# Adding products of zeros to TensorE's message sums in 47 steps of a graph network kernel

## The chip, the core and the metric

The kernel runs on one core of one Trainium2 chip. The metric is the device time of one execution in microseconds (us). The core has five engines with queues of their own: TensorE (PE in the profile, with its weight loads as PEld), VectorE (DVE), ScalarE (ACT), GpSimd (POOL) and SyncE (SP). Engines wait for each other by semaphores.

## What is computed

The reference is one message passing block (PaiNN) on a graph of 1250 nodes with 512 features and 40000 edges, sorted by destination, then a residual addition and a layer norm:

```python
x_j = x[src]
v_j, s_j = x_j[:, :384].reshape(E, 128, 3), x_j[:, 384:]
s_j = silu(s_j @ W1 + b1) @ W3 + b3
edge_basis = rbf * cutoff @ W2 + b2
split = s_j * edge_basis
s1, s2, s3 = split[:, :128], split[:, 128:256], split[:, 256:]
v_msg = v_j * s1[:, :, None] + s3[:, :, None] * edge_attr1[:, None, :]
x = x + segment_sum(concat([v_msg, s2]), dst)
...
x = x + segment_sum(msg, dst)
return layernorm(x_in + x)
```

The first sum runs over messages of edges. For the second one, each node's message is made once per node, and the sum over edges is a product with a matrix of link counts, which the kernel gathers on the way.

## The kernel before

A table of 640 numbers per node is made first and kept in DRAM. Then the function `windowed` goes over the edges in batches of up to 4 x 128, some 80 steps of one batch each; four batches make a group, and a group's sums cover a window of 128 rows of destinations. For a batch, GpSimd gathers 128 rows four times (L782), three steps ahead. A step does the following.

- `messages(t)` on DVE: the one-hot matrix `hot` (L877) from `eb`, then the products of gathered rows and edge factors (L949, and L952 as the last reader of `eb`), with `spread` (L891) between them, then `pair` (L968).
- `add_messages(t - 1)` on TensorE: for each of the four tiles j a product of `hot` and the messages into rows 32j to 32j + 31 of the PSUM bank `agg` (L984), then twelve smaller products with `spread` (L990). In the changed kernel these are L987 and L998.
- `count_links(t - 1)` on TensorE: four f16 products of `one` and `pair` (L1013), 160 columns each, into the bank `adj`. The accumulator carried between groups comes in by L1005.
- `edge_factors(t + 1)` on TensorE: the edge factors of the next batch into `eb` (L938, four f32 products of 388 columns, eight records in the trace). There is one bank set `eb`, so this waits until DVE has read the last one.
- `gather(t + 3)`, the gathers for three steps on, whose first waits for `eb`.

Between these, tables (`first`, `early`, `late`, `dve`, `mid`, `amid`), filled by `at(when, step, rank, fn)`, put the work on finished groups and nodes: copying sums (`close_group`), joining two groups (`sum_block`, L1080), the node update (`times_u`, L1148, whose result ScalarE copies as `vu`; `times_uv`, L1159; `over_parts`, L1175), the basis transposes (L855) and the second sum (`begun`, L1388). Each engine works through its own list in the order in which the code issues it. The work repeats every eight steps, two groups being one block of nodes. Steps count from 0; the first starts some 30 us into the span.

The code around the change, in `add_messages`:

```python
for j in js:
    nc.tensor.matmul(
        agg[j * WIN : (j + 1) * WIN, :], hots[t][:, j, :],
        msg[:, j, :width], start=(i == 0), stop=False, skip_group_check=True,
    )
for c in range(3):
    for j in js:
        nc.tensor.matmul(
```

`sh.number` is an f16 tile of 128x256 that holds 0 to 255 in each row; `WIN` is 32 and `P` is 128.

Of the kernel before, what the change touches and what calls it, by code (L numbers as in the profile page):

```python
# [12 lines left out]
F16 = mybir.dt.float16  # L13
# [8 lines left out]
P = 128  # L22
# [18 lines left out]
WIN = SHARE + 2 * MARGIN  # L41
# [9 lines left out]
GROUP = 4  # L51
LEAD = 3
LAG = 2


def by_component(ap):
# [8 lines left out]
def gnn_resnorm(  # L65
# [31 lines left out]
    nc = tc.nc  # L97
# [8 lines left out]
    sh = Shared()  # L106
# [6 lines left out]
    const = ctx.enter_context(tc.tile_pool(name="const", bufs=1))  # L113
# [147 lines left out]
    for k in range(2):  # L261
# [4 lines left out]
        sh.number, pattern=[[1, 2 * P]], base=0, channel_multiplier=0,  # L266
        allow_small_or_imprecise_dtypes=True,
    )
    sh.basis = const.tile([P, TPC * CPG, FEAT], F32, name="basis")
    nc.gpsimd.memset(sh.basis[:, :, N_RBF:], 0.0)  # L270
    nc.gpsimd.memset(sh.basis[:, :, N_RBF], 1.0)
# [360 lines left out]
def windowed(tc, sh):  # L632
# [13 lines left out]
    nc = tc.nc  # L646
# [24 lines left out]
    def tiles(g, i):  # L671
        return [j for j in range(CPG) if lanes(g, i, j)]
# [14 lines left out]
    def last_tile(g, j):  # L687
        return max(i for i in range(TPC) if lanes(g, i, j))
# [7 lines left out]
    with tc.tile_pool(  # L696
        name="msg", bufs=4
    ) as pool, tc.manual_schedule(), ExitStack() as banks:

        number = sh.number  # L700
# [277 lines left out]
        def add_messages(t):  # L978
            g, i = batches[t]
            if i == 0:  # L980
                aggs[g] = ps_sum.tile([P, width], F32, name="agg")
            agg, msg, js = aggs[g], msgs.pop(t), tiles(g, i)
            for j in js:
                nc.tensor.matmul(  # L984
                    agg[j * WIN : (j + 1) * WIN, :], hots[t][:, j, :],
                    msg[:, j, :width], start=(i == 0), stop=False, skip_group_check=True,
                )  # L987
            for c in range(3):
                for j in js:
                    nc.tensor.matmul(  # L990
                        agg[j * WIN : (j + 1) * WIN, c * C : (c + 1) * C],
                        spread[t][:, j, c, :], msg[:, j, width:],
                        start=False, stop=(i == last_tile(g, j) and c == 2),
                        skip_group_check=True,
                    )
# [752 lines left out]
        for t in range(max(*first, *early, *late, *dve, *mid) + 1):  # L1748
            if t < NT:
                messages(t)  # L1750
            if t == NT - 4:
                assert all(len(tiles(*batches[u])) == CPG // 2 for u in range(NT - 3, NT))
                made_in[NT - 3], made_in[NT - 2] = new_banks("halves", [CPG // 2] * 2)
                made_in[NT - 1] = made_in[NT - 3]
            if t == NT - 1:
                out_banks.update(zip(in_factors, new_banks("out", [1] * CPG), strict=True))
            run(first, t)
            if 1 <= t <= NT:
                add_messages(t - 1)
                if t not in behind:  # L1760
                    count_links(t - 1)
            run(early, t)
            if t + 1 < NT - 2:
                made = edge_factors(t + 1)
            if t + 1 in (NT - 3, NT - 2):
                edge_factors(t + 2)
            if t + ahead < NT:
                gather(t + ahead, made if t + ahead < NT - 2 else None)
            if t in behind:
                count_links(t - 1)  # L1770
            run(mid, t)
            run(late, t)
            run(dve, t)
# [38 lines left out]
def _general(ctx, tc, sh):  # L1812
# [170 lines left out]
    def edge_sums(table, sums, begin, finish, add, pool, ps_agg):  # L1983
# [13 lines left out]

        for step in range(NT + LAG):
            t = step
            if t < NT:  # L2000
# [9 lines left out]
                nc.vector.tensor_scalar(hots[t], lane, slots[:, t, 4:5], None, op0=ALU.is_equal)  # L2010
            t = step - LAG
            if t >= 0:
# [134 lines left out]
```

## Time and profile before

| what | value |
|---|---|
| median of 3 runs | 572.19 us (569.93 to 572.43) |
| the profiled execution | 573.55 us |
| its span, first to last instruction | 571.7 us |
| mean granted TensorE clock in it | 0.881 of 2.4 GHz |
| PE busy | 456.2 us (80%), 4260 matmuls |
| DVE, ACT, POOL busy | 424.5 us, 380.3 us, 336.2 us |
| moved by DMA | 123.29 MB, mean 216 GB/s |

The span is what the trace covers; the execution's time has a little more around it. A busy share is an average over the whole span. In a timeline row the number after the start is the time from the start of the first merged instruction to the end of the last, "xN" counts the merged instructions, and the bracket gives the engine's idle time before the first one and what ended it. "issue" means that the profile shows nothing that ended it. The granted clock is what the throttle allowed TensorE, as a share of full speed.

### The profile page before, as it was taken

What the parts mean: (1) busy time and instruction counts of PE and PEld (TensorE: products, weight loads), DVE (VectorE), ACT (ScalarE), POOL (GpSimd) and SP (SyncE); (2) the same over time, 40 slices, a digit from 0 to 9 for tenths busy, and PEclk for the clock granted to TensorE, in tenths of its full rate; (3) what the DMA queues carried; (4) which work ended last, traced back from release to release, by engine and by line L of the source; (5) the groups of instructions that cost most, each with busy time, mean ns of one, the idle gap of its engine ahead of it and who ended that gap; (6) DMA issues with size and microseconds to landing.
All of it is one profiled execution on the core that took longest, in us unless ns stands there. A gap on an engine that the chain in (4) does not pass through costs nothing.

```text
span 571.7 us, 11259 instructions
## 1 busy us (share of the span) xinstructions
PE 456.2 (80%) x4260; PEld 256.5 (45%) x4260; DVE 424.5 (74%) x672; ACT 380.3 (67%) x976; POOL 336.2 (59%) x363
## 2 busy tenths in 40 slices
PE   9556787887878798687888788798879697899993
PEld 6322343453444354344534444454445364455672
DVE  6785877767876777687777877777767867797775
ACT  4675467485767657577856767695749566787664
POOL 8375656656655665666566665656555655664530
PEclk9757787878979887988889898999879998989998
DMA  8896777777777677777677778777766776877414
GB/s 267 288 284 180 214 229 217 218 217 228 212 234 200 222 211 200 239 216 210 204 243 213 236 223 235 203 229 239 234 196 201 214 206 204 253 214 230 178 37 148
DMA packets 37840, 123.29 MB, mean 216 GB/s; under 512 B 7141, under 2 KB 9815, under 8 KB 37779
## 3 DMA queue, kind: packets, MB, share of 16 engines
q0 software_dynamic: 25568, 104.34, 61.3%
q1 hardware_dynamic: 11010, 17.51, 9.5%
q8 instruction: 35, 0.57, 0.4%
q10 hardware_dynamic: 1200, 0.66, 0.4%
q14 instruction: 27, 0.21, 0.1%
HBM read 112.97 MB, written 9.51 MB: 214 GB/s over the span
## 4 chain that ended last, share of the span: by engine, by line
PE 70%; ACT 10%; DVE 9%; issue 9%; DVEq 0%; another core or an unknown queue 0%; ACTq 0%
PE eb L938 14%; PE agg L984 13%; PE agg L990 8%; PE adj L1013 5%; PE begun L1388 4%; ACT one L913 3%; PE work L1080 3%; PE work L855 3%; PE work L1175 2%; DVE more L952 2%; PE work L1159 2%; DVE nodes L952 2%; ACT one L903 2%; PE work L1224 1%; DVE more L949 1%
## 5 line engine op out<-in xcount | busy, mean ns | idle before, releaser
L782 POOL DMA_INDIRECT more<-table,src_i x189 | 184.7, 977 | 118.6 <-issue 42.7
L782 POOL DMA_INDIRECT nodes<-table,src_i x124 | 120.9, 975 | 79.6 <-issue 28.7
L913 ACT ACTIVATE one<-one,weight,src_f 128x128 f16<-128x128 f16 x313 | 128.5, 482 | 0.2
L938 PE MATMUL eb<-w_sb,basis_t 25*128 25x388 f32 x614 | 80.6, 584 | 58.7 <-issue 43.7
L903 ACT ACTIVATE one<-number,low 128x128 f16<-128x128 f16 x313 | 99.8, 392 | 16.6 <-PE adj L1013 10.0
L877 DVE TENSOR_TENSOR hot<-lane,eb 128x128 f32<-128x128 f32 (+1 forms) x78 | 22.1, 284 | 101.5 <-PE eb L938 61.5
L952 DVE TENSOR_TENSOR more<-more,eb 128x1536 f32<-128x1536 f32 (+2 forms) x48 | 81.8, 1705 | 0.0
L984 PE MATMUL agg<-more,hot 128*32 128x512 f32 x378 | 65.2, 704 | 2.6 <-issue 1.9
L938 PEld LDWEIGHTS eb<-w_sb,basis_t 25*128 25x128 f32 x614 | 27.0, 195 | 81.0 <-issue 59.8
L949 DVE TENSOR_TENSOR more<-more,eb 128x1024 f32<-128x1024 f32 (+2 forms) x48 | 56.9, 1186 | 2.5 <-issue 2.5
L990 PEld LDWEIGHTS agg<-more,spread 128*32 128x32 f32 x1134 | 41.9, 122 | 34.1 <-issue 32.9
L952 DVE TENSOR_TENSOR nodes<-nodes,eb 128x1536 f32<-128x1536 f32 x30 | 52.4, 1747 | 0.0
L990 PE MATMUL agg<-more,spread 128*32 128x128 f32 x1134 | 50.5, 300 | 0.3 <-issue 0.3
L984 PE MATMUL agg<-nodes,hot 128*32 128x512 f32 x248 | 41.4, 685 | 2.6 <-issue 1.5
L891 DVE TENSOR_TENSOR spread<-hot,eb 128x384 f32<-128x384 f32 (+1 forms) x78 | 42.1, 541 | 0.0
L1013 PE MATMUL adj<-pair,one 128*128 128x160 f16 x313 | 37.4, 239 | 3.3 <-ACT turn L819 1.1
L968 DVE TENSOR_TENSOR pair<-number,column 128x640 f16<-128x640 f16 (+1 forms) x81 | 38.7, 478 | 0.0
L949 DVE TENSOR_TENSOR nodes<-nodes,eb 128x1024 f32<-128x1024 f32 x30 | 36.4, 1214 | 0.0
L990 PEld LDWEIGHTS agg<-nodes,spread 128*32 128x32 f32 x744 | 25.8, 119 | 22.4 <-issue 21.8
L860 ACT COPY basis_t<-work 128x512 f32<-128x512 f32 x20 | 11.7, 586 | 35.4 <-PE work L855 27.1
L990 PE MATMUL agg<-nodes,spread 128*32 128x128 f32 x744 | 31.5, 292 | 0.1
L1013 PEld LDWEIGHTS <-one 128*128 128x128 f16 x313 | 22.0, 101 | 20.1 <-issue 16.8
(296 smaller groups left out, 730.1 us busy)
## 6 DMA issues: line engine op xcount, KB each, us to landing
table<-more SPq DMA_DIRECT2D x10, 320.0 KB
more<-table,src_i POOLq DMA_INDIRECT x189
spilled<-begun SPq DMA_DIRECT2D x10, 256.0 KB
more<-spilled SPq DMA_DIRECT2D x2, 1280.0 KB
node_x<-in_x_dram SPq DMA_DIRECT2D x35, 64.0 KB
nodes<-table,src_i POOLq DMA_INDIRECT x124
out_dram<-more SPq DMA_DIRECT2D x7, 256.0 KB
nodes<-in_x_dram POOLq DMA_DIRECT2D x2, 768.0 KB
```

What stands on the lines that cost most here:

```text
L782: got = nc.gpsimd.indirect_dma_start(out=rows_t[:n, j, :], out_offset=None, in_=sh.table1, in_offset=bass.IndirectOffsetOnAxis(ap=sh.src_i ...
L891: nc.vector.tensor_mul(spread[t][:m, js], hots[t][:m, js, None, :].to_broadcast(shape), factors_of(t, js)[:m, :, V : V + 3, None].to_broad ...
L903: nc.scalar.activation(onehots[t][:, j, :], number[:, :P], AF.Abs, bias=low[:, e : e + 1])
L913: nc.scalar.activation(one, one, AF.Relu, scale=less[:, e : e + 1], bias=worth[:, e : e + 1])
L938: made = nc.tensor.matmul(made_in[t][:, j, : V + CARRY], turned[g][rows, i, :], sh.w2_sb[rows, :], start=True, stop=True,)
L949: nc.vector.tensor_mul(msg[:m, js, V:], msg[:m, js, V:], factors_of(t, js)[:m, :, C:V])
L952: nc.vector.tensor_mul(msg[:m, js, :V].rearrange("p t (k c) -> p t k c", k=3), msg[:m, js, :V].rearrange("p t (k c) -> p t k c", k=3), fac ...
L968: nc.vector.tensor_tensor(pair[:m, js, :].rearrange("p t (l h) -> p t l h", h=2), number[:m, : PARTS * WIN].rearrange("p (l h) -> p l h", ...
L984: nc.tensor.matmul(agg[j * WIN : (j + 1) * WIN, :], hots[t][:, j, :], msg[:, j, :width], start=(i == 0), stop=False, skip_group_check=True,)
L990: nc.tensor.matmul(agg[j * WIN : (j + 1) * WIN, c * C : (c + 1) * C], spread[t][:, j, c, :], msg[:, j, width:], start=False, stop=(i == la ...
L1013: nc.tensor.matmul(to[:, :, at : at + WIN], one[:m, j, :], pair[:m, j, :].rearrange("e (p n) -> e p n", n=WIN), start=(i == 0 and j == js[ ...
L1388: nc.tensor.matmul(acc, casts[a, b], rows[:, a, :], start=(start and a == first and k == 0), stop=(stop and a == end - 1 and k == 1),)
```

## The change

Between the four products with `hot` and the twelve with `spread` of a batch, TensorE gets a number of f16 products more: the stationary operand is a tile of zeros (128x32), the moving one is `number` (256 columns), and the result is added to rows 0 to 31 and columns 0 to 255 of `agg`. The sums therefore keep their values. How many come is read from the table `IDLE` by the step modulo 8; `add_messages(t)` is called in step t + 1, so the products of a step stand under its own number modulo 8. From step 48 on there are none. The zeros are set once by GpSimd.

```diff
+IDLE = 10, 0, 5, 5, 8, 5, 0, 10
...
+    sh.zero = const.tile([P, WIN], F16, name="zero")
+    nc.gpsimd.memset(sh.zero, 0.0)
...
                     msg[:, j, :width], start=(i == 0), stop=False, skip_group_check=True,
                 )
+            for _ in range(IDLE[(t + 1) % len(IDLE)] if t < 47 else 0):
+                nc.tensor.matmul(
+                    agg[:WIN, : 2 * P], sh.zero, number, start=False, stop=False,
+                    skip_group_check=True,
+                )
             for c in range(3):
```

On TensorE, in step 5 of the kernel before (the transposes L855 make the next group's basis):

```order
L984 MATMUL agg<-nodes,hot 32x512 x4
L990 MATMUL agg<-nodes,spread 32x128 x12
L855 MATMUL work<-ident,basis 128x128 x4
L938 MATMUL eb_396<-w_sb,basis_t 128x388 x4
L1005 MATMUL adj<-passed,ident 128x5x16
```

The same place in the changed kernel, whose lines from here on have higher numbers (L992 is the added product):

```order
L987 MATMUL agg<-nodes,hot 32x512 x4
L992 LDWEIGHTS zero
L992 MATMUL agg<-number,zero 32x256
L992 LDWEIGHTS zero
L992 MATMUL agg<-number,zero 32x256
...
L998 MATMUL agg<-nodes,spread 32x128 x12
L858 MATMUL work<-ident,basis 128x128 x4
L941 MATMUL eb_398<-w_sb,basis_t 128x388 x4
L1013 MATMUL adj<-passed,ident 128x5x16
```

Five pairs of a weight load and a product have come between `hot` and `spread`; nothing else moved. In the steps of phases 0 and 7 there are ten such pairs in this place, and in those of phase 4 eight.

On GpSimd, the memset stands among the constants set at the start, well ahead of the gathers:

```order
L266 IOTA number 128x256
L271 MEMSET zero 128x32
L273 MEMSET basis 128x16x12
L274 MEMSET basis 128x16
```

The row of `zero` is new; the queues of the other engines hold the same rows as before.

## Rows read from the trace of the kernel before

**Rows 1.** The page's part 1: busy us, share of the span, instructions.
```profile
PE 456.2 (80%) x4260; PEld 256.5 (45%) x4260; DVE 424.5 (74%) x672; ACT 380.3 (67%) x976; POOL 336.2 (59%) x363
```

**Rows 2.** Who waited for whom: us in total, times, longest us.
```profile
DVE hot L877 <- PE eb L938: 61.5, 32, 4.8
```

**Rows 3.** Stretches, steps 2-7 and blocks of eight: us, busy by engine, PEclk, DMA share, GB/s.
```profile
48.00:84.75 36.75, 27.07 (x297) 13.20 (x297) 29.42 (x45) 18.64 (x55) 23.27 (x24) 0.83 0.73 210
84.75:134.76 50.01, 39.83 (x403) 21.08 (x400) 36.76 (x52) 33.32 (x86) 31.07 (x32) 0.81 0.74 219
134.76:185.47 50.71, 40.85 (x414) 21.58 (x413) 38.34 (x55) 34.48 (x90) 31.22 (x32) 0.87 0.74 219
185.47:236.91 51.44, 41.93 (x418) 23.16 (x416) 38.35 (x56) 34.66 (x90) 30.85 (x32) 0.87 0.72 215
236.91:288.15 51.24, 39.74 (x416) 22.12 (x414) 38.30 (x55) 34.47 (x90) 31.24 (x32) 0.87 0.73 217
288.15:337.72 49.57, 40.47 (x411) 21.82 (x409) 38.33 (x56) 35.14 (x91) 31.24 (x32) 0.93 0.77 229
```

**Rows 4.** Timeline of DVE, steps 32 and 33.
```profile
236.91 0.29 DVE L877 TENSOR_TENSOR hot<-lane,eb 128x128 f32<-128x128 f32 x1 [1.38 <-PE work L1224]
...
238.71 1.75 DVE L952 TENSOR_TENSOR more<-more,eb 128x1536 f32<-128x1536 f32 x1
...
243.03 0.29 DVE L877 TENSOR_TENSOR hot<-lane,eb 128x128 f32<-128x128 f32 x1 [1.70 <-PE eb L938]
```

**Rows 5.** Timeline of PE, steps 31 to 34.
```profile
232.26 0.45 PE L1013 MATMUL adj<-pair,one 128*128 128x160 f16 x4
234.42 0.93 PE L938 MATMUL eb<-w_sb,basis_t 25*128 25x388 f32 x8 [1.71 <-issue]
...
240.51 1.56 PE L938 MATMUL eb<-w_sb,basis_t 25*128 25x388 f32 x8 [2.51 <-DVE more L952]
...
249.96 0.45 PE L1005 MATMUL adj<-passed,ident 128*128 128x80 f32 x2 [2.39 <-ACT adj L835]
```

**Rows 6.** Timeline of PE, steps 36 to 38.
```profile
266.97 0.93 PE L938 MATMUL eb<-w_sb,basis_t 25*128 25x388 f32 x8 [2.27 <-issue]
269.07 1.65 PE L1159 MATMUL work<-uv,x_t 128*128 128x128 f32 x6 [1.16 <-ACT vu L1152]
270.65 1.94 PE L984 MATMUL agg<-more,hot 128*32 128x512 f32 x8
...
274.84 0.93 PE L938 MATMUL eb<-w_sb,basis_t 25*128 25x388 f32 x8
...
277.44 1.07 PE L984 MATMUL agg<-more,hot 128*32 128x512 f32 x8
```

**Rows 7.** Stretches: steps 13, 21, 29, 37, 45, then 24 with 25, then 34.
```profile
115.44:122.47 7.03, 6.59 (x51) 3.89 (x52) 5.08 (x7) 5.00 (x15) 3.81 (x4) 0.59 0.76 227
165.70:173.14 7.44, 7.00 (x51) 4.12 (x52) 5.08 (x7) 5.23 (x15) 3.79 (x4) 0.55 0.74 223
217.39:224.59 7.20, 6.78 (x51) 3.92 (x52) 5.08 (x8) 4.99 (x15) 3.82 (x4) 0.57 0.74 218
268.65:275.84 7.19, 6.77 (x51) 3.91 (x52) 5.08 (x7) 4.98 (x15) 3.79 (x4) 0.57 0.76 228
319.05:325.28 6.23, 5.86 (x54) 3.46 (x55) 5.08 (x8) 5.01 (x15) 3.81 (x4) 0.73 0.73 213
185.47:198.81 13.34, 10.04 (x85) 4.49 (x79) 10.04 (x16) 9.10 (x24) 7.70 (x8) 0.87 0.73 231
249.17:256.30 7.13, 6.34 (x57) 3.96 (x58) 4.95 (x7) 3.98 (x13) 4.03 (x4) 0.76 0.74 226
```

**Rows 8.** The page's part 5, L1013: busy us, mean ns of one, idle before.
```profile
L1013 PE MATMUL adj<-pair,one 128*128 128x160 f16 x313 | 37.4, 239 | 3.3 <-ACT turn L819 1.1
```

**Rows 9.** Timeline of POOL, its start.
```profile
9.74 0.13 POOL L271 MEMSET basis<- 128x16 f32 x1
...
23.30 1.14 POOL L782 DMA_INDIRECT more<-table,src_i  x1 [7.29 <-DVE turn L805]
```

## The prediction

> **What bounds the kernel now.** I read the page first. TensorE (PE) is busy 456.2 of 571.7 us [rows 1], the busiest engine, but busy is not bound, so the question is which wait ends last in a step. In the list of waits the longest is VectorE (DVE) waiting with its first instruction of a step, the hot comparison, for the edge factors `eb`: 61.5 us in 32 waits [rows 2]. So DVE waits for PE. I then cut the loop into blocks of eight steps, the period of the table IDLE, by the starts of hot. Phase below is the step modulo 8, and the fillers, as I call the new products, stand in steps 1 to 47. The blocks of steps 8 to 47 take 50.01, 50.71, 51.44, 51.24 and 49.57 us at a granted clock of 0.81, 0.87, 0.87, 0.87 and 0.93 [rows 3]. Taking every moment as either 1.2 or 2.4 GHz, a mean of 0.87 is 26% of the time at 1.2 GHz, and the six blocks hold 78 us of it (twice the missing share times the length, summed).
>
> Third, two steps in the timelines. In step 32 hot starts at 236.91, and the last DVE instruction that reads `eb`, L952, ends at 240.46, so 3.55 us later. PE, idle for 2.51 us, starts the next `eb` at 240.51, and hot of step 33 follows only 2.52 us behind that, at 243.03 [rows 4, 5]. One step before, PE had idled 1.71 us and `eb` ran from 234.42 to 235.35 by the profile, yet hot of step 32 came 2.49 us after its start [rows 4, 5]. Step 32 takes 6.12 us. So a step has a **floor of about 6.13 us** that neither PE's work nor its clock sets: something holds back the signal that hot waits for, and I can't tell what. In step 37 it is otherwise: hot starts at 268.65, L952 would end 3.55 us later at 272.20, but `eb` starts only at 274.84, and hot follows 1.00 us behind, at 275.84 [rows 6, 7]. There PE is the bound and the step takes 7.19 us. An `eb` may therefore come some 1.5 us late (2.5 less 1.0) before anyone notices. Only the steps in which it comes later than that can win or lose.
>
> **Where the clock costs time.** Step 37 (phase 5) is the pattern. Before it PE idles 2.27 us, runs one `eb`, idles 1.16 us for ScalarE's copy of `vu`, and then runs the step at 1.2 GHz: eight hot products take 1.94 us, against 1.07 one step on [rows 6]. The phase 5 steps 13, 21, 29 and 37 take 7.03, 7.44, 7.20 and 7.19 us at clocks of 0.55 to 0.59; step 45, at 0.73, takes 6.23 [rows 7]. These four are 28.86 - 4 x 6.23 = 3.94 us longer than step 45's length would make them. Steps 24 and 25 together take 13.34 us [rows 7], where steps 32 and 33 take 249.17 - 236.91 = 12.26 [rows 4, 7]; that is 1.08 us more. Step 34 (phase 2) takes 7.13 [rows 7], after PE waited 2.39 us in front of L1005 [rows 5].
>
> **The change part by part.** By the table there are 248 fillers: ten in each of 5 steps of phase 0 and 6 of phase 7, eight in each of 6 of phase 4, five in each of 6 of phases 2, 3 and 5, none in phases 1 and 6.
>
> Price of one: the nearest row is the other f16 product, L1013. Four of them with 160 columns take 0.45 us [rows 5] and one alone 0.239 [rows 8], so each further one adds (0.45 - 0.239) / 3 = 0.070 us. For 256 columns that is 0.112 us at 2.4 GHz and 0.225 at 1.2. The bounds are 0 (hidden beside products that write other rows of `agg`) and 0.239 x 256 / 160 = 0.38. I take 0.112, since all fillers write the same 32 rows and so queue behind each other. Sum: 248 x 0.112 = 27.8 us of PE time. The Trainium skill, "TensorE: Matmul & The Clock Gate", section "Wait — 56ns, not 53.3ns?", states N / 2.4 GHz + 2.5 ns from start to start, which would be 109 ns for one and 27.1 us for all; no more hangs on it.
>
> Where it lies: ten are 1.12 us, inside the idle 1.71 and 2.51 us of phases 7 and 0 [rows 5]. Eight are 0.90, inside the 2.27 us before phase 5 [rows 6]. If this cover were gone, the 1.5 us of tolerance would still hold them. Five in phase 3 are 0.56, within the same tolerance. All of these I cost at nothing. In a group's last batch the fillers also hold up the `agg` sums that ScalarE copies, by 0.90 to 1.12 us; that copy feeds L1080 behind `eb`, in a step with the same slack. Phases 2 and 5 have no sure cover: five add 0.56 us there at 2.4 GHz and 1.12 at 1.2. DVE, ScalarE and the queues get no instruction. GpSimd gets one memset of 128x32, about the 0.13 us of its neighbour, which its later 7.29 us of idleness before the first gather hides [rows 9]. The zeros are long there when the first filler needs them, so no new wait arises.
>
> What the fillers can return: they turn idle PE time into busy time where the clock falls afterwards. In phase 4 the 2.27 us of idleness shrinks to 1.37; but the 1.16 behind `eb` stays, as does the 2.39 in front of L1005, since the fillers stand behind hot. So I expect the half-clock stretch of phase 5 to vanish in most steps and not in all. Forecast: -3.94 for the four steps, -1.08 for steps 24 and 25, +0.98 because one of the four keeps its stretch, +0.84 for step 34 (the middle of 0.56 and 1.12). **Sum -3.2 us.** The profiled execution took 573.55 us (span 571.7 and 1.85 around it), so 570.4; it stands 1.36 above the median of the runs, 572.19, which becomes **569.0**. The ends of the uncertain terms: all four and step 34 relieved gives -6.0; none relieved and five fillers at 1.2 GHz in each gives the slower rival.
>
> **The rivals.**
>
> *The fillers land on the path (slower).* Place: steps 13, 21, 29, 37 and 45 (phase 5) and 34 (phase 2), where PE is the bound. If the clock there stays at 1.2 GHz, because the rest of the idleness is enough to lower it, or because products of 32 columns with zeros do not raise it (so that the change does not do what it says), each pays 5 x 0.225 = 1.12 us: 6.7 us, 578.9. It decides where `eb` starts more than 1.5 us after L952's end. For it: the gap of 1.16 is untouched and follows at once. Against it: 0.90 us of the gap before it goes. Chance 0.13.
>
> *The clock rises and nothing follows (no change).* Most of the 78 us lies in steps that sit on the 6.13 us floor anyway. If two or three of the phase 5 steps are relieved (-2 to -3) and the fillers cost 0.56 in phases 2 and 5 elsewhere (four or five of them), the balance is 572. For it: the block at clock 0.81 is faster than those at 0.87 [rows 3]. Chance 0.28.
>
> *Every step of steps 8 to 47 reaches the floor.* Five blocks at 8 x 6.13 = 49.04 are 245.2 against 252.97: -7.8, 564.4. For it: the block at 0.93 comes within 0.5 us of that. Against it: the untouched waits of phases 2 and 5. Chance 0.12.
>
> *All half-clock time comes back in proportion.* If PE's work set every step, 78 us at 1.2 GHz would shrink to 39, giving 533. Against it: the floor, which PE meets with 1.71 and with 2.51 us of idleness, and the block at 0.81, which is not the longest. Chance 0.02. The Trainium skill, same page, sections "Terms" and "HAM oscillation — how this bites in real kernels", puts the penalty of a lowered clock at the lowered time x (1 - K/N), which is this reading; the trace speaks against it here.
>
> **How the numbers follow.** The forecast has 0.45. One half per cent, 2.9 us, is about what a measurement of this kernel tells from no change; the forecast lies just beyond it, so of its 0.45 I put 0.33 on faster and 0.12 on no change. Faster: 0.33 + 0.12 + 0.02 = 0.47. Same: 0.12 + 0.25 of the second rival = 0.37. Slower: 0.13 + 0.03 = 0.16. The range runs from the floor rival's 564.4, rounded to 564.5, to 575.0, which takes in the no-change case and the mild part of the slower one (two or three steps paying 1.12).
>
> **What would show it.** Right: the clock of the blocks of steps 16 to 47 rises to 0.93 or more; phase 5 steps measure about 6.2 with hot products near 1.07 us; a filler adds 0.11 us; phases 7 and 0 keep 6.1 us while PE's idleness before `eb` shrinks by 1.1. Wrong: phase 5 steps of 8 us with fillers at 0.22 apart (first rival); a raised clock with blocks as long as now (second); steps well below 6.1 us (fourth, and my floor would be PE's after all). If the signal that hot waits for comes later where fillers run, the floor itself hangs on PE and every filled step loses.

## The result and the profile after

The changed kernel took 586.79 us (median of six runs, 583.57 to 592.95) against 572.32 before on the same chip: a ratio of 1.0247, 95% interval 1.0206 to 1.0288. It is **slower**, by 14.5 us, where I had forecast 3.2 us faster. The execution that was profiled with this result was a disturbed one (its span is 591.1 us), so the rows below are from a later run of the same kernel, with a ratio of 1.030. The execution profiled there took 581.91 us, the shortest of its five (median 589.79), so its rows hold only part of the loss.

The page's part 1 of the changed kernel, against [rows 1]:
```profile
PE 470.2 (81%) x4508; PEld 270.2 (47%) x4508; DVE 424.2 (73%) x672; ACT 379.0 (65%) x976; POOL 337.2 (58%) x364
```
Its waits (us in total, times, longest), against [rows 2]:
```profile
DVE hot L880 <- PE eb L941: 62.4, 35, 4.4
...
PEld work L1167 <- ACT vu L1160: 24.5, 8, 4.0
ACT sums L1034 <- PE eb L941: 23.6, 5, 5.2
```
For the last one, the kernel before has:
```profile
ACT sums L1026 <- PE eb L938: 5.0, 1, 5.0
```
TensorE is busy for 14 us more, DVE and ScalarE as long as before. L1167 (L1159 before) waits longer for `vu`, and one wait has grown: ScalarE's for the sums of a group, L1034 (L1026 before). Put down to any releaser, it was about 20 us in all and is about 36.

Stretches of the changed kernel: the five blocks of steps 8 to 47, then steps 13, 21, 37, 18 (columns as in [rows 3]; the column behind POOL is the granted clock):
```profile
85.62:137.87 52.25, 42.23 (x438) 23.75 (x438) 36.73 (x52) 32.99 (x86) 31.05 (x32) 0.87 0.71 210
137.87:193.02 55.15, 42.93 (x455) 25.11 (x450) 38.30 (x55) 34.17 (x90) 31.22 (x32) 0.88 0.68 200
193.02:244.38 51.36, 44.48 (x448) 24.85 (x443) 38.28 (x56) 34.66 (x90) 31.36 (x32) 0.93 0.72 216
244.38:296.38 52.00, 44.91 (x461) 25.46 (x462) 38.30 (x56) 34.05 (x90) 31.67 (x32) 0.93 0.72 214
296.38:350.04 53.66, 45.16 (x452) 25.44 (x446) 38.35 (x55) 34.83 (x91) 31.22 (x32) 0.87 0.71 212
...
116.52:125.52 9.00, 7.07 (x56) 4.27 (x57) 5.08 (x8) 6.46 (x19) 3.80 (x4) 0.62 0.61 185
172.09:180.63 8.54, 6.61 (x56) 3.91 (x57) 5.08 (x8) 6.47 (x19) 3.79 (x4) 0.64 0.62 194
277.15:284.00 6.85, 5.12 (x56) 3.18 (x57) 5.07 (x7) 5.98 (x18) 3.79 (x4) 1.00 0.74 221
...
150.29:159.67 9.38, 8.17 (x62) 5.05 (x63) 4.95 (x8) 4.40 (x14) 4.02 (x4) 0.64 0.55 170
```
The clock did rise: 0.81 became 0.87 in the first block and 0.87 became 0.93 in two others, while the last fell from 0.93 to 0.87 [rows 3]. Yet every block but the third is longer, by 0.8 to 4.4 us. The time sits in a few steps: 13 and 21 took 7.03 and 7.44 us before [rows 7] and take 9.00 and 8.54; step 37 takes 6.85 at full clock, less than its 7.19 before but more than a step on the floor (the 6.1 us of the prediction); step 18 takes 9.38 where it took 6.24. Most other steps keep their length.

**Where the new time begins.** ScalarE in steps 20 and 21 before:
```profile
162.67 0.58 ACT L1026 COPY sums<-agg 128x512 f32<-128x512 f32 x1 [1.45 <-PE work L1148]
164.13 0.23 ACT L1048 COPY passed<-adj 128x80 f32<-128x80 f32 x1 [0.87 <-remote]
...
165.61 0.48 ACT L1152 COPY vu<-work 128x384 f32<-128x384 f32 x1 [0.23 <-PE eb L938]
```
and TensorE there:
```profile
160.14 0.82 PE L990 MATMUL agg<-nodes,spread 128*32 128x128 f32 x12
...
166.14 1.65 PE L1159 MATMUL work<-uv,x_t 128*128 128x128 f32 x6 [1.18 <-ACT vu L1152]
```
The same of the changed kernel, ScalarE first:
```profile
171.87 0.59 ACT L1034 COPY sums<-agg 128x512 f32<-128x512 f32 x1 [4.32 <-PE eb L941]
172.35 0.23 ACT L1056 COPY passed<-adj 128x80 f32<-128x80 f32 x1
172.46 0.54 ACT L1058 ACTIVATE high<-adj,shifts 128x320 f32<-128x320 f32 x1
173.04 0.56 ACT L1061 ACTIVATE counts<-high,shifts 128x320 f16<-128x320 f32 x1
173.51 0.46 ACT L1160 COPY vu<-work 128x384 f32<-128x384 f32 x1
```
```profile
132.31 1.15 PE L992 MATMUL agg<-number,zero 128*32 128x256 f16 x9
...
166.43 0.90 PE L998 MATMUL agg<-nodes,spread 128*32 128x128 f32 x23
...
174.02 1.65 PE L1167 MATMUL work<-uv,x_t 128*128 128x128 f32 x6 [2.73 <-ACT vu L1160]
175.60 1.94 PE L987 MATMUL agg<-more,hot 128*32 128x512 f32 x8
177.31 1.04 PE L992 MATMUL agg<-number,zero 128*32 128x256 f16 x4
```
Hot of step 20 starts at 160.44 before and at 166.76 after. Counted from it, the copy of the sums starts at 2.23 and at 5.11 us, 2.9 us later, although by the profile's modelled ends the last product of `agg` ends at 0.52 and at 0.57. ScalarE stood idle for 4.32 us before it. Four copies later it reaches `vu`, whose products end at 168.4 by the profile; L1167 starts 1.93 us behind hot of step 21 (172.09) where L1159 started 0.44 behind it (165.70), TensorE idles 2.73 us in place of 1.18, and the step runs on at 1.2 GHz.

### The profile page after: what moved, and what is told of

Its sections match the earlier page's. It is cut to its first block, busy times and chain, and to the rows that moved or that the text cites. A ratio compares the mean times of both kernels' runs of the same rounds, so it can differ in the third digit from the quotient of the medians.

```text
span 591.1 us, 11756 instructions
## 1 busy us (share of the span) xinstructions
PE 473.0 (80%) x4508; PEld 274.7 (46%) x4508; DVE 424.5 (72%) x672; ACT 379.2 (64%) x976; POOL 336.2 (57%) x364
## 4 chain that ended last, share of the span: by engine, by line
PE 69%; DVE 10%; issue 9%; ACT 8%; DMA 3%; another core or an unknown queue 0%; DVEq 0%; SPq 0%
PE eb L941 14%; PE agg L987 13%; PE agg L998 8%; PE adj L1021 5%; PE begun L1396 4%; PE agg L992 4%; DVE more L955 3%; PE work L1183 3%; PE work L1088 3%; ACT one L916 2%; PE work L1167 2%; PE work L858 2%; DMA nodes<-in_x_dram 2%; DVE more L952 2%; PE work L1232 2%
## 5 line engine op out<-in xcount | busy, mean ns | idle before, releaser
L941 PE MATMUL eb<-w_sb,basis_t 25*128 25x388 f32 x614 | 79.4, 556 | 46.9 <-issue 33.4
L987 PE MATMUL agg<-more,hot 128*32 128x512 f32 x378 | 68.8, 712 | 4.0 <-ACT counts L1061 2.5
L998 PEld LDWEIGHTS agg<-more,spread 128*32 128x32 f32 x1134 | 39.8, 118 | 19.9 <-issue 18.9
L987 PE MATMUL agg<-nodes,hot 128*32 128x512 f32 x248 | 43.7, 691 | 5.0 <-ACT sums L1034 1.8
L992 PEld LDWEIGHTS <-zero 128*32 128x32 f16 x248 | 26.6, 109 | 27.8 <-issue 23.8
L992 PE MATMUL agg<-number,zero 128*32 128x256 f16 x248 | 39.2, 305 | 0.3 <-issue 0.3
L998 PE MATMUL agg<-nodes,spread 128*32 128x128 f32 x744 | 34.6, 301 | 0.0
```

Of the source, the lines that this page charges most:

```text
L941: made = nc.tensor.matmul(made_in[t][:, j, : V + CARRY], turned[g][rows, i, :], sh.w2_sb[rows, :], start=True, stop=True,)
L987: nc.tensor.matmul(agg[j * WIN : (j + 1) * WIN, :], hots[t][:, j, :], msg[:, j, :width], start=(i == 0), stop=False, skip_group_check=True,)
L992: nc.tensor.matmul(agg[:WIN, : 2 * P], sh.zero, number, start=False, stop=False, skip_group_check=True,)
L998: nc.tensor.matmul(agg[j * WIN : (j + 1) * WIN, c * C : (c + 1) * C], spread[t][:, j, c, :], msg[:, j, width:], start=False, stop=(i == la ...
```

## The experiments

Phase and fillers are used as in the prediction: the step modulo 8, and the added products. **Theory A:** the fillers in a group's last batch (phases 0 and 4) hold up the sums; ScalarE takes its work in order, so `vu` (phase 4) and the fades (phase 0) come late, and the step behind is long. **Theory B:** the fillers' own time is the loss, where TensorE is the bound. Ratios are to the kernel before, timed on the same chip.

**1. One part at a time** (one chip, 564.5 us before).

> The changed kernel once more, for a profile at its usual time. All theories: 584 to 589 us against 572 before, ratio about 1.025. In the first profile of the changed kernel steps 5, 13, 21, 29, 37 and 45 (phase 5) are 8.8 us longer together than before, steps 18 and 34 4.0 longer, and the rest near 6.1 as before; I expect the same here.

> The fillers of phase 4 are left out, all others stay. Theory A (the eight fillers of phase 4 hold up the last sums of a group; ScalarE takes its copies in order, so the copy of vu comes late, and the phase 5 step runs long): the phase 5 steps go back to 7.0 to 7.4 us plus at most 1.1 for their own five fillers, so 5 to 9 us of the 14.5 come back, 578 to 582 us. Theory B (the fillers' own TensorE time is the loss, where TensorE is the bound, in phases 2 and 5): nothing comes back, and with less work before phase 5 its clock falls no later: 586 to 589. Theory C (any filler ahead of a group's last sums costs, phase 0 as much as phase 4): 580.


```
-IDLE = 10, 0, 5, 5, 8, 5, 0, 10
+IDLE = 10, 0, 5, 5, 0, 5, 0, 10
```


> Only the eight fillers of phase 4, 48 products in all instead of 248. Theory A: the phase 5 steps are as long as in the changed kernel less their own fillers, 8 to 9 us each at a late vu: 578 to 580 us, over half of the loss from a fifth of the products. Theory B: 48 products in a phase where TensorE has idle time cost nothing: 571 to 573. Theory C: 577 to 580.


```
+IDLE = 0, 0, 0, 0, 8, 0, 0, 0
```


> All fillers stay; in phase 4 ScalarE's copy of vu is put ahead of the copies that close the group (TensorE's order is the same). Theory A: vu no longer waits for the sums, its copy starts about 1.4 us earlier against the next hot, the gap before L1167 shrinks from 2.7 to about 1.3 us, and the five phase 5 steps give back 1.4 each: 579 to 581 us. Theory B: the copy's place does not matter, 586 to 588. If the signals of TensorE come late as a whole and not in ScalarE's order, then vu is late by itself and at most 2 us come back.


```
-                    (early, 4, 1, times_u), (late, 4, 1, times_uv), (late, 5, 1, lengths),
+                    (early, 4, -1, times_u), (late, 4, 1, times_uv), (late, 5, 1, lengths),
```
| kernel | us | ratio (95%) | steps 13, 21, 29, 37, 45 together |
|---|---|---|---|
| as changed | 581.50 | 1.030 (1.022 to 1.038) | 42.4 |
| none in phase 4 | 571.88 | 1.011 (1.001 to 1.021) | 33.0 |
| phase 4 alone | 571.09 | 1.013 (1.003 to 1.022) | 37.6 |
| all, `vu` first | 567.82 | 1.007 (1.003 to 1.011) | 33.0 |

The kernel before has 35.1 us in these five steps [rows 7]. Taking the 48 fillers of phase 4 away gives 9.6 us back, of a loss of 17.0 on this chip; those alone cost 6.6. With every filler in place, ScalarE's order alone gives 13.7 back, more than the 7 I expected. Theory B falls as the main cause. Steps 37 and 18 without fillers in phase 4:
```profile
271.46:277.64 6.18, 5.22 (x61) 3.31 (x61) 5.08 (x8) 4.07 (x13) 3.81 (x4) 1.00 0.78 229
146.73:156.19 9.46, 8.18 (x62) 5.05 (x63) 4.95 (x7) 4.47 (x14) 4.03 (x4) 0.64 0.57 172
```
Step 37 reaches the floor at full clock with its own five fillers still in it, which therefore cost nothing there: what I had forecast for phase 5 does happen once `vu` is on time. Step 18, the second step behind phase 0, is at 9.46 here. In the changed kernel (the run shown above), ScalarE and then TensorE up to that wait in step 18:
```profile
143.99 0.58 ACT L1037 COPY sums<-agg 112x512 f32<-112x512 f32 x1 [4.60 <-PE work L1088]
...
151.24 0.20 ACT L838 COPY adj<-fade 128x64 f32<-128x64 f32 x1
```
```profile
151.50 0.72 PE L1013 MATMUL adj<-passed,ident 128*128 128x80 f32 x2 [2.53 <-ACT adj L838]
```
Behind the late sums of step 16 ScalarE works through its queue without a pause up to the fades, on which L1013 waits 2.53 us, and the clock falls in a step in which TensorE is the bound. The same wait was 2.39 us in step 34 before [rows 5]. So this part of theory A is not shown to come from the fillers: as changed on the chip of these four kernels, steps 18 and 34 took 6.17 and 6.87 us, where I had expected 4.0 us more than before, and with fillers in phase 4 alone step 18 still took 7.04.

**2. Both copies of ScalarE moved ahead, with and without fillers.** The first four ran on a chip on which the kernel before takes 478 us, not 565 to 575. I call chips like this one the second kind, the others the first.

> The kernel before once more, for a profile from the same chip as the other runs. All theories: a ratio of 1, and the phase 5 steps 13, 21, 29 and 37 between 7.0 and 7.5 us.

> The kernel before, without fillers, with ScalarE's copy of vu ahead of the copies that close the group. Theory A (what counts in phase 5 is when vu comes, not the fillers): the gap of 1.16 us in front of L1159 closes, the steps 13, 21, 29, 37 go from 7.0 to 7.4 towards 6.2, and 61 and 69 (9.33 and 7.50 before) also gain: 4 to 7 us in all, ratio 0.988 to 0.993. Rival (the clock falls before eb in any case, without fillers): vu earlier gives at most the gap itself, and the ratio is 0.995 to 1.0.

> As the last, and ScalarE's copy of the fades (steps 17, 33, 49, 65) moved ahead of the one-hot work of its step, so that the first counts of the next step do not wait for it. Theory A': ScalarE's order is what makes steps 18, 34, 50 and 66 long (6.23, 7.13, 6.58 and 8.14 us before), and they go to 6.1: 2 to 4 us below the last kernel, ratio 0.982 to 0.988. Rival (another wait ends a little later in front of the same products): no difference from the last kernel.


```
-            at(early, 4 * g - 3, 6, bring_fades, g)
+            at(first, 4 * g - 3, 8, bring_fades, g)
```


> All fillers, with both of ScalarE's copies moved. Theory A': all that the fillers lost came by ScalarE's order; with vu first alone this was 1.007 of before, with steps 18, 34 and 66 still at 8.2 us; those go to about 6.2, 5 to 6 us less: ratio 0.995 to 0.999. If the fillers have a price of their own, this stays above the kernel with both moves and no fillers by 5 us or more; if the clock they keep up is worth something, it is at or below it.

There all are alike: 1.001 (0.998 to 1.004), 1.000 (0.997 to 1.003) and 1.002 (0.999 to 1.005); the expectations, made for the other kind of chip, missed. The next three ran on a chip with 574.9 us before.

> The changed kernel again, beside the two kernels with ScalarE's copies moved, on one chip. The last call ran on a chip on which the kernel before took 478 us instead of 564 to 572, and where hot follows eb's end after 0.13 us (median) instead of 1.26. If this is a chip of the first kind: ratio 1.025 to 1.03. If of the second: theory A says that the loss came by late signals of TensorE to ScalarE, and where signals are not late it goes: 0.998 to 1.006. Theory B (the fillers' own time): 1.01 or more there, since TensorE is nearer to being the bound.

> No fillers, both copies of ScalarE moved ahead. On a chip of the second kind 0.997 to 1.003, as measured. On one of the first kind theory A': 4 to 10 us faster than before, 0.982 to 0.993, since the phase 5 steps and 18, 34, 50 and 66 go to 6.2. Rival (without fillers the clock falls all the same): 0.995 to 1.0.

> All fillers, both copies moved. Second kind of chip: 1.002 as measured. First kind: with vu first alone it was 1.007 with the steps 18, 34 and 66 at 8.2 us; theory A' brings these to 6.2: 0.995 to 0.999, and if fillers are worth anything at equal order of ScalarE it is at or below the kernel without fillers; if they cost by themselves, 5 us or more above it.

The changed kernel: 589.79 us, 1.030 (1.025 to 1.034). Both moves without fillers: 565.18, **0.986 (0.982 to 0.990)**. Both moves with all fillers: 569.38, 0.992 (0.989 to 0.995). Steps 8 to 47 and step 18, without fillers:
```profile
86.28:336.16 249.88, 199.51 (x2022) 107.79 (x2024) 189.92 (x273) 170.78 (x447) 155.59 (x160) 0.90 0.75 222
...
148.70:154.95 6.25, 4.31 (x51) 2.79 (x42) 4.95 (x7) 4.22 (x13) 4.02 (x4) 1.00 0.73 212
```
and with all of them:
```profile
85.20:338.26 253.06, 210.23 (x2239) 120.42 (x2237) 189.90 (x272) 170.46 (x447) 156.04 (x160) 0.94 0.74 220
...
148.11:154.38 6.27, 5.89 (x64) 3.79 (x64) 4.95 (x8) 3.85 (x12) 4.01 (x4) 1.00 0.69 206
```
Step 18 is at the floor in both, and so are 34, 50 and 66 (6.2 to 6.3 us in all eight), where the other seven profiles from the first kind in this document have 6.15 to 9.46 us: the late fades were the cause. What the move of `vu` alone gives without fillers was not run on the first kind. At equal order the fillers raise the clock from 0.90 to 0.94 and buy nothing; the stretch is 3.2 us longer. The four executions without fillers took 564.80 to 566.06 us and the ten with them 566.62 to 572.13: they do not overlap, and the medians are 4.2 us apart, so on this chip the fillers cost by themselves, if less than the 5 us I had set as the mark. In ScalarE's old order they cost 14.9 us there (589.79 against 574.94), in the new one 4.2: between 10 and 11 us of the loss went through ScalarE's queue. The moves alone gain 9.8 us without any filler, so the 13.7 of the first experiment is not all loss undone. The Trainium skill, "TensorE: Matmul & The Clock Gate", sections "Terms" and "HAM oscillation — how this bites in real kernels", prices a lowered clock at the lowered time x (1 - K/N); as an estimate by that, going from 20% to 12% of the stretch would gain 10 us. These two rows speak against it for a loop whose steps TensorE mostly does not bound.

**3. How late by a filler.**

> Fillers in phase 4 alone, 1, 1, 2, 3, 4 and 6 of them in steps 4, 12, 20, 28, 36 and 44. It asks how late the sums' copy comes by a filler. Theory of proportion: 0.11 to 0.22 us later for each, so 0.1 to 1.3 us. Theory of steps (first kind of chip): TensorE's signal is let go only at certain moments about 1.45 us apart, so the copy stays at 2.2 us after hot for few fillers and jumps to 3.7 or 5.1 at some count between 2 and 6. On a chip of the second kind: in proportion.

This is one execution, on the first kind, with one step for each count. `vu` starts 5.8 us behind hot with one filler (step 12) and 5.2 with two (step 20), as before the change (5.79 and 5.17 in the same steps), 6.2 with three and with four, and 6.7 with six, in steps that had 5.1 to 5.2 before. It jumps between two and three fillers, the third being 0.11 us of work, and does not grow in proportion; the theory of steps holds for `vu`. The sums' own copy jumped less regularly: 2.9, 2.3, 3.7, 2.9 and 5.1. Fillers are not the only thing that makes it late: in steps 52, 60 and 68 of the kernel before, which has none, it starts 3.7, 5.8 and 3.7 us behind hot.

**4. The second kind of chip, and what holds the signals.**

> Fillers in phases 2, 3, 5 and 7 alone (none in 0 and 4, the phases in which a group of batches ends), ScalarE's order as it was. Theory A (the loss is the delay of a group's last sums): 0.99 to 1.00 on a chip of the first kind, since phase 5 with its fillers but without those of phase 4 was 2 us shorter than before in the second experiment, and the steps 18 and 34 stay as before. Theory B (the fillers cost where they stand): phases 2 and 5 pay up to 1.1 us each in 11 steps, 1.01 to 1.02. On a chip of the second kind: 0.998 to 1.004 by A.

> The kernel before with fewer gathers: three for each step, not four, in steps 21 to 28, two in 29 to 36, one in 37 to 44; the rows left out keep what was there, so the messages of those batches are not the reference's. Theory G (the late signals of TensorE hang on the gathers that are under way): on a chip of the first kind the time from eb's end to hot, 1.26 us in the median, falls with each gather left out, to about 0.1 us with one, and the steps go from 6.1 to 4.6 to 5 us. Rival (they are late whatever GpSimd does): it stays near 1.3 and the steps near 6.1. On a chip of the second kind nothing changes but a little.


```
             for j in tiles(g, i):
+                if 24 <= t < 48 and j >= 4 - (t - 16) // 8:
+                    continue
```


> The changed kernel a third time, to have it on a chip of the second kind if this is one. First kind: ratio 1.025 to 1.03. Second kind: theory A says the loss goes with the late signals, 0.998 to 1.006; theory B 1.01 or more.

> Fillers in phases 2, 3, 5 and 7 alone, for a chip of the first kind. Theory A: 0.99 to 1.00 there. Theory B: 1.01 to 1.02. On a chip of the second kind 1.000 as measured in the last call.

> Three, two and one gathers for each step in steps 21 to 28, 29 to 36 and 37 to 44, for a chip of the first kind; the messages of those batches are not the reference's. Theory G: the time from eb's end to hot falls from 1.3 us to about 0.1 with one gather, and the steps from 6.1 to between 4.6 and 5. Rival: it stays near 1.3 and the steps near 6.1. On a chip of the second kind the steps 37 to 44 stay between 4.6 and 5.7, as in the last call.

> Both of ScalarE's copies moved ahead, and fillers in phases 2, 3, 5 and 7 alone. On a chip of the first kind: if fillers away from the group ends are worth anything, this is below the 0.986 of both moves without fillers; if they are worth nothing, 0.984 to 0.990; if they cost by themselves, 0.992 as with all fillers. Second kind: 0.998 to 1.003.

All six ran on chips of the second kind (478.3 and 477.8 us before). **The changed kernel there: 1.001 (0.998 to 1.004).** Fillers in phases 2, 3, 5 and 7 alone: 1.000 twice; those with both moves: 1.001 (0.998 to 1.005). Fewer gathers: 470.8 and 470.1 us, with hot about 0.1 us behind `eb` as it was. So whether the gathers hold TensorE's signals on the first kind, the question of these two runs, was **not tested** there, and neither was what fillers in phases 2, 3, 5 and 7 alone do there.

The profiles of the first kind bear on it all the same. Two gathers of the kernel before, in steps 31 and 37:
```profile
234.82 1.00 POOL L782 DMA_INDIRECT nodes<-table,src_i  x1 [0.30 <-issue]
...
272.63 0.95 POOL L782 DMA_INDIRECT nodes<-table,src_i  x1 [0.30 <-issue]
```
The first is under way when `eb` ends at 235.35 [rows 5]; hot follows at 236.91 [rows 4], 1.56 us behind `eb` and 1.09 behind the gather. The second has long ended, at 273.58, when `eb` ends at 275.77 [rows 6]; hot follows at 275.84, after 0.07 us. The other steps agree. In nine profiles from this kind (the kernel before and eight of the experiments) I take the steps 2 to 77 in which VectorE had idled over 0.2 us before hot. In 365 of them a gather is under way at the end of `eb`, and hot comes 1.54 us behind in the median. In 98 the last gather had ended over 1.2 us before, and hot comes at most 0.08 us behind. In the 108 between it comes 0.75 us behind in the median. Before the first gather, at 23.30 us [rows 9], VectorE and ScalarE follow TensorE by 0.04 us here too (fifteen waits in the kernel before). On the second kind hot comes at most 0.08 us behind with a gather under way as well (149 steps of eight profiles).

The copy of the sums in step 20 fits this. The second gather of that step before, and the fourth in the changed kernel:
```profile
161.04 0.95 POOL L782 DMA_INDIRECT more<-table,src_i  x1 [0.30 <-issue]
```
```profile
169.87 0.95 POOL L785 DMA_INDIRECT more<-table,src_i  x1 [0.30 <-issue]
```
The copy starts 0.68 us behind the end of the one and 1.05 behind the end of the other; with fillers in phase 4 alone, 0.80 behind the third. The gathers follow each other every 1.25 us. That they hold the signals is what these profiles suggest; no run shows it, since none left gathers out on this kind, and why one copy is let go behind the second gather and another behind the fourth stays **open**.

What the second kind shows is the change without late signals. The kernel before, step 20 (hot at 136.62), TensorE and ScalarE:
```profile
137.09 0.84 PE L990 MATMUL agg<-nodes,spread 128*32 128x128 f32 x24
...
141.07 0.94 PE L1159 MATMUL work<-uv,x_t 128*128 128x128 f32 x6
```
```profile
138.00 0.59 ACT L1026 COPY sums<-agg 128x512 f32<-128x512 f32 x1 [0.27 <-PE agg L990]
...
139.64 0.46 ACT L1152 COPY vu<-work 128x384 f32<-128x384 f32 x1
```
The changed kernel, step 20 (hot at 134.39):
```profile
135.68 0.90 PE L998 MATMUL agg<-nodes,spread 128*32 128x128 f32 x21
...
139.90 0.94 PE L1167 MATMUL work<-uv,x_t 128*128 128x128 f32 x6
```
```profile
136.66 0.59 ACT L1034 COPY sums<-agg 128x512 f32<-128x512 f32 x1 [1.30 <-PE agg L998]
...
138.30 0.46 ACT L1160 COPY vu<-work 128x384 f32<-128x384 f32 x1
```
The copy follows the last product by 0.07 and 0.08 us. Eight fillers move it from 1.38 to 2.27 us behind hot: 0.89, as I had costed them. `vu` ends 4.37 us behind hot, ahead of the `eb` before L1167 (139.04), and L1167 follows that `eb` with no wait. The delay I had forecast is there and does no harm.

## Why the prediction was wrong

**The step that failed** is the sentence that in a group's last batch "the fillers also hold up the `agg` sums that ScalarE copies, by 0.90 to 1.12 us; that copy feeds L1080 behind `eb`, in a step with the same slack". It has two faults. The consumer was incomplete: in phase 4 the copy stands four places ahead of `vu` in ScalarE's queue, and `vu` ends the wait of L1159, which I had called untouched [rows 6]; in phase 0 it stands ahead of the fades and L1005 [rows 5], though that fillers made these later is not shown. And the size was wrong on this kind of chip: not 0.90 but 2.9 us in step 20, 1.4 in the same step with the fillers of phase 4 alone. By this way between 10 and 11 of the 14.9 us were lost on the chip with 574.9 us before; the other 4.2 are the fillers' own, and which steps they fall in was not singled out.

How the phase 5 steps come about is best seen over nine profiles from chips of the first kind (the kernel before and eight of the experiments), eight such steps each (13 to 69), by whether L1167 (L1159) starts within 0.5 us behind hot, or 0.8 to 1.9 us behind it, and by the granted clock of the step (mean us, number of steps):

| | clock 0.95 or more | 0.7 to 0.9 | below 0.68 |
|---|---|---|---|
| `vu` on time | 6.21 (12) | 6.59 (20) | 7.36 (7) |
| `vu` late | 6.85 (1) | 7.42 (18) | 8.54 (14) |

I had the clock right (7.36 to 6.21 is the 1 us of my term for each step) and left the other row out. The change moved steps up in the clock and down to late.

**The other steps.** The price of a filler was right: nine take 1.15 us at 2.4 GHz where one takes 0.27, so 0.11 each, and four take 1.04 at 1.2 GHz where one takes 0.42, so 0.21. Phases 7 and 0 took 6.2 to 6.5 us from step 7 on (6.0 to 6.2 before), close to the nothing I had costed, but for step 24, which is shorter before and after (4.98 and 4.60). The sum of the gains did not come: the steps at the floor do not follow the clock, as my second rival said. The four phase 5 steps, from which I took 3.94 us off, went from 28.9 to 30.6 in the run shown (two gained, two lost more) and to 32.9 in the first experiment. Steps 24 and 25 took 13.5 us, not 1.08 less than 13.34, and step 34 took 6.93, not 0.84 more than 7.13. The first rival had the right sign and steps with another mechanism: its condition, that `eb` starts late and the clock stays low, came true in part of the steps, by `vu` and not by the fillers' own 1.12 us. With `vu` on time at full clock the five fillers cost nothing; in steps both late and below 0.68 the changed kernel has 8.5 to 9.5 us in phase 5 where fillers stand and 7.2 to 8.5 with those of phase 4 alone, so there they may cost up to a microsecond; this is not shown, since step 61 of the kernel before, without a filler, takes 9.33 there too. The floor of 6.13 us I had called unexplained is one of this kind of chip: it is 4.6 on the other. Nor is it a bound of every step here: phases 3 and 4 take 7.1 and 5.3 us, and step 24 even less.

## What to carry to other kernels

Filler work is not free merely because the engine is idle where it goes: look at which result it is put in front of, and at everything that stands behind that result's consumer in the consumer's queue. Where two unrelated results wait in one in-order queue, put the one whose reader sets the end first; here two copies moved were worth 1.4% on one kind of chip, where the fillers lost 2.5 to 3.0%. A raised clock was worth something only in the steps that TensorE bounds. And time such a change on more than one chip: the same one was 1.025 to 1.030 in three measurements on one kind and 1.001 on the other.

## What I had not expected of the hardware

The same program runs in two ways, by the chip: 565 to 575 us, or 478. The instructions off TensorE take the same time in both (a gather on GpSimd 977 and 975 ns in the mean, DVE busy for 424.5 and 422.6 us); what differs is when a result of TensorE is seen. From the end of `eb` to hot it is 1.2 us in the median of the kernel before on the first kind and 0.13 on the second; from the last product of `agg` to the copy of the sums in step 20, 1.71 and 0.07. DMA moved 216 GB/s on the first and 259 on the second, which may be cause or effect. Under the fillers the 1.71 became 4.5 although the product ended at the same time behind hot, and in step 20 the copy's start was found at 2.2, 3.6 or 5.1 us behind hot, not between, in the kernels with ScalarE's order as it was. These moments lie 0.7 to 1.1 us behind the ends of gathers, and the delay is gone where no gather is near; that the gathers cause it, and why only on one kind of chip, was not tested, since the kernel with fewer gathers ran on the second kind alone.
